# Five groups of transposed tiles ahead of the products, and row sums kept on chip in eight tiles

## The chip, the cores and the metric

The kernel runs on one core of one Trainium2 chip. The metric is the device time of one execution in microseconds; three runs of the kernel before gave 5170.29, 5173.07 and 5176.02 us, median 5173.07 us. A separate, profiled execution took 5216.56 us, and its trace spans 5214.8 us on the core.

## The reference

Two layers on a batch of 32 images of 128 channels and 56 x 56 pixels, all in f32.

```python
# layer 0: depthwise 7x7 convolution, layer norm, a mixture of 8 experts, skips
x = conv7x7_depthwise(input) + bias;  x = layernorm(x) * gamma + beta
topv, topi = top_k(xf @ Wg + bg, 2)          # xf: one row of 128 numbers for each pixel
wts = softmax(topv);  order = argsort(-wts[:, 0])
# in that order each pixel takes a slot in its two experts while they have room (cap)
h = gelu(eb @ W1 + b1);  y = h @ W2 + b2     # per expert, on the rows of its slots
moe = sum over the two slots of gate * y[slot]
return input + x + layer_scale * moe
# layer 1: 3x3 convolution (dilation 3), batch norm, gelu, then in the frequency domain
feat = gelu(batchnorm(conv2d(x, conv_w)))
F2 = fft2(feat);  qkv = F2.reshape(B, 8, 8, N)
attn = softmax over the real part and over the imaginary part of (q conj(k) * tau)
out_f = abs(ifft2(attn @ v))
gate = sigmoid(cg2(gelu(batchnorm(cg1(F2.real))))) * F2
y = concat([out_f, abs(ifft2(gate))]);  return y + x
```

## The kernel before, in words

Layer 0 comes first. The convolution runs on TensorE and leaves normalized rows in the DRAM tensor `xf`; a search finds each expert's threshold; then the eight experts run one after the other, in chunks of 512 rows. A chunk's rows are gathered (L1048), transposed (L1054, L1055), multiplied by W1 (`ph`, L1071) and by W2 (`py`, L1089), scaled, and stored to the DRAM tensor `yf` (L1115). The last expert reads rows that were put in order earlier and has no gathers of its own.

The images of layer 1 are worked in 16 pairs. A pair has seven blocks of eight pixel rows, 112 blocks in all. Before a block can be used, its sum must be made: the block's rows of `xf` (tile `xa`, 448 KB) plus the outputs of the two experts of each pixel, which are gathered from `yf` by 14 indirect DMAs on GpSimd (L458), seven into each of two `y` tiles. Three functions control this.

- `release` (L442) asks for one more gather. Every gather gets a wait on a TensorE instruction: that which was the last when the gather `leash` places before it was asked for. `leash` is 4 in the last expert and 16 in layer 1. The first gather of a block also issues the load of `xa`.
- `total` (L465) makes a block's sum with two VectorE additions (L474). It first asks for what is still missing of the block's 14 gathers. In the kernel before it then stores the sum to the DRAM tensor `xsum` (L475).
- `bring` (L490) makes sure that a block's sum was made, by calling `total` until it is, and in the kernel before loads it back from `xsum` into an `xs` tile (L497), of which there are three.

`release` is called from two places. In the last expert, `ahead` calls it at each tick, for as many blocks as the stored rows of `yf` allow. In layer 1, `worked` counts the columns that TensorE was given and calls `release` once for each `PACE` of 684.2 columns, then `totals(7)`, which makes the sum of a block once seven gathers beyond its own were asked for.

Layer 1 itself has a `front` and a `back` for each pair. `front` takes a block at a time: `place` transposes the block's sum (`pxs`, L1289) and adds it to the padded image (L1293), `bring` is called for the block two further on, and then come 18 of the convolution's matmuls by twos, in three lots of `taps` (`pf`, L1304), and a gelu into `feat` (L1312). `back` makes four transforms, two forward and two inverse. Each calls `transform` (L1339), which works in groups of four tiles: `turn` transposes a group (`pt`, L1347) and VectorE copies it to a `mid` tile (L1334); `product` multiplies the group by a constant matrix (`pm`, L1355) and ScalarE copies the result out (L1358). Three turned groups are made before the first product; from there on one turn and one product take turns. Between the second and the third transform, `attend` makes the attention's products (`pre` and `pim`) and a gate is worked out (`pq`).

The order on TensorE is the program's. While `back` of a pair runs, the main loop feeds it steps of the next pair's `front` in proportion to the columns done, and three lots of taps at a place where a transform needs all of the one before it. Five PSUM banks serve `pt`, `pm`, `pxs`, `pre`, `pim` and `pq` in turn. The `mid` tiles share a pool of six buffers each with the output tiles (`ring`).

Of the kernel before, what the change touches and what calls it, by code (L numbers as in the profile page):

```python
# [30 lines left out]
F32 = mybir.dt.float32  # L31
# [7 lines left out]
C = 128  # L39
# [6 lines left out]
E = 8  # L46
# [5 lines left out]
NB = H // P8  # L52
# [22 lines left out]
def conv_seq_kernel(ctx: ExitStack, tc: tile.TileContext, t: dict, out: bass.AP, dbg: dict):  # L75
# [28 lines left out]

    xf = dram.tile([J * 128, C], F32, name="xf")
    yf = dram.tile([NSLOT + 1, C], F32, name="yf")
    xs_ = dram.tile([J * 128, C], F32, name="xsum")
    xl = dram.tile([-(-cap // 512) * 512, C], F32, name="xlast")
    xfv = xf.rearrange("(j p) c -> p j c", p=128)
    xsv = xs_.rearrange("(j p) c -> p j c", p=128)  # L110
    xlv = xl.rearrange("(j p) c -> p j c", p=128)


# [306 lines left out]
    begun_ = {}  # L420
    marks = []
    leash = {"n": 4}
    made_ = {"asked": 0, "summed": 0, "rows": 0}
    rows = {}
    step = {}
    work = {"since": 0}
# [15 lines left out]
    def release():  # L442

        n = made_["asked"]
        if n >= NRB * NG:
            return
        made_["asked"] += 1
        r, k = divmod(n, NG)
        if k == 0:
            xs = d6.tile([128, NB, C], F32, name="xa", tag="xa")  # L450
            nc.sync.dma_start(out=xs, in_=xfv[:, r * NB : (r + 1) * NB, :])
            begun_[r] = xs, []
        if k % NB == 0:
            begun_[r][1].append(d6.tile([128, NB, C], F32, name="y"))
        m = k % NB
        s = (slot1, slot2)[k // NB]
        marks.append(step["pe"])
        gated(marks[max(0, n - leash["n"])], nc.gpsimd.indirect_dma_start(  # L458
            out=begun_[r][1][-1][:, m, :],
            out_offset=None,  # L460
            in_=yf[: 1 + reach(r), :],
            in_offset=bass.IndirectOffsetOnAxis(ap=s[:, r * NB + m : r * NB + m + 1], axis=0),
        ))

    def total():  # L465

        r = made_["summed"]
        while made_["asked"] < (r + 1) * NG:
            release()
        made_["summed"] += 1  # L470
        xs, ys = begun_.pop(r)
        with tc.issue_after(step["dve"].ins):
            for y in ys:
                nc.vector.tensor_tensor(out=xs, in0=xs, in1=y, op=ALU.add)  # L474
        nc.sync.dma_start(out=xsv[:, r * NB : (r + 1) * NB, :], in_=xs)  # L475

    def totals(lag):

# [9 lines left out]
            totals(NB)  # L488

    def bring(r):  # L490
        if r >= NRB or r < made_["rows"]:
            return
        made_["rows"] = r + 1
        while made_["summed"] <= r:
            total()
        xs = rows[r] = d3.tile([128, NB, C], F32, name="xs")
        nc.sync.dma_start(out=xs, in_=xsv[:, r * NB : (r + 1) * NB, :])  # L497

    def inputs(pr):
        xps = [d4.tile([C, XL], F32, name="xp") for i in range(2)]  # L500
# [24 lines left out]
    if True:  # L525
# [649 lines left out]
        for e in range(E):  # L1175
            todo = late
            chain["on"] = e >= early
            if e + 1 < E:
                todo = todo + [due(1.4, lambda e=e: scale(e + 1))]
            if e in pairs:  # L1180
                todo = todo + search(*pairs[e])
            if e == E - 1:
                for s in late:
                    s()
                locate()
                lists_.close()
                rkey.__exit__(None, None, None)
                d4 = ctx.enter_context(tc.tile_pool(name="d4", bufs=4))
                d6 = ctx.enter_context(tc.tile_pool(name="d6", bufs=6))
                d3 = ctx.enter_context(tc.tile_pool(name="d3", bufs=3))  # L1190
                d0 = ctx.enter_context(tc.tile_pool(name="d0", bufs=1))
                first_inputs = inputs(0)
                bC = load(d0, "beta", [C, 1], t["ln_beta"].rearrange("(c o) -> c o", o=1))
                eps5 = d0.tile([128, 1], F32, name="eps5")
                norms = [[load(d0, n, [128, 5], t[n])] for n in ("bn1", "cgbn")]
                for i, n in enumerate(norms):
                    n += [d0.tile([128, 1], F32, name=f"{k}{i}") for k in ("scale", "shift")]
                cw = load(d0, "cw", [C, 9, DD], t["conv_w"])
                g1 = load(d0, "g1", [128, 32], t["cg1"])
                g2 = load(d0, "g2", [128, 128], t["cg2"])  # L1200
                g2b = load(d0, "g2b", [128, 1], t["cg2_b"])
                tau = load(d0, "tau", [128, 1], t["tau"])
                neg = load(d0, "neg", [128, 128], t["neg"])
                meanw = load(d0, "meanw", [128, 128], t["meanw"])
                rw = load(d0, "rw", [2 * W, 4 * KF], t["rw"])
                rh = load(d0, "rh", [2 * H, 4 * KF], t["rh"])
                ih = load(d0, "ih", [4 * KF, 2 * H], t["ih"])
                iw = load(d0, "iw", [4 * KF, 2 * W], t["iw"])
                todo = []
            if e + 1 < E - 1:  # L1210
                ids2, gates2 = lists()
                steps, late = listing(e + 1, ids2, gates2)
                todo = todo + steps
            elif e + 1 < E:
                (ids2, gates2), late = last, []
            if e == 0:
                todo = todo + search(E - 1, 1)
            if e == early - 1:
                last = [c1.tile([128, NC], d, name=n) for d, n in ((I32, "ids_last"), (F32, "gates_last"))]
                steps, done_ = listing(E - 1, *last)  # L1220
                todo = todo + steps + done_
            slots_ = len(chunks) * 4 - 18
            state = [0, 0, 0.0, 0]
            whole = sum(share.get(f, 0.7) for f in todo)

            def tick():
                state[0] += 1
                if e == E - 1:
                    state[2] += 1
                    ahead(i, state[2])  # L1230
                with tc.issue_after(step["dve"].ins):
                    while state[1] < len(todo) and state[2] * slots_ < state[0] * whole:
                        s = todo[state[1]]
                        if s in apart and state[3] == state[0]:
                            break
                        s()
                        state[2] += share.get(s, 0.7)
                        state[1] += 1
                        state[3] = state[0]

            for i, c0 in enumerate(chunks):
                if i + 1 < len(chunks):
                    then = fetch(ids, chunks[i + 1], e == E - 1)
                elif e + 1 < E:
                    then = fetch(ids2, 0, e + 1 == E - 1)
                if early <= e < E - 1 and i + (e - early) * len(chunks) < NC:
                    put(0, i + (e - early) * len(chunks))
                state[2] = 0 if e == E - 1 else state[2]
                if e == E - 1 and i == len(chunks) // 2:
                    batchnorms()  # L1250
                if e == E - 1 and i == len(chunks) - 1:
                    for r in range(2):
                        bring(r)
                ns, xT = now
                hT, gelu, mine = first_layer(e, ns, xT, tick)
                if left:
                    after, more = second_layer(*left, tick)
                    after(gelu)
                    mine = mine + more
                spots.append(mine + mine[-1:] * (8 - len(mine)))  # L1260
                left = e, c0, gates, ns, hT
                now = then
            assert state[1] == len(todo)
            if e + 1 < E:
                ids, gates = ids2, gates2
# [7 lines left out]
    d1 = ctx.enter_context(tc.tile_pool(name="d1", bufs=1))  # L1273
    d2 = ctx.enter_context(tc.tile_pool(name="d2", bufs=2))
    ring = ctx.enter_context(tc.tile_pool(name="ring", bufs=6))
    psum = ctx.enter_context(tc.tile_pool(name="psum_d", bufs=5, space=PSUM))
    psumf = ctx.enter_context(tc.tile_pool(name="psum_f", bufs=2, space=PSUM))
    psum1 = ctx.enter_context(tc.tile_pool(name="psum_g", bufs=1, space=PSUM))
# [2 lines left out]

    def place(r, xps):
        xs, rb = rows.pop(r), r % NB
        for m0 in range(0, NB, 4):
            nm = min(4, NB - m0)
            pt = bank("pxs")
# [52 lines left out]
    def transform(src, n, m, by, to, copy, more=None):  # L1339
# [3 lines left out]
        def turn(i0):  # L1343
            ni = min(4, n - i0)
            pt = bank("pt")
            for i in range(ni):
                step["pe"] = nc.tensor.transpose(pt[:m, i * 128 : (i + 1) * 128], src(i0 + i), ident)  # L1347
            mid = ring.tile([128, 4, 128], F32, name="mid")
            dve(mid[:m, :ni, :].rearrange("p i c -> p (i c)"), pt[:m, : ni * 128])
            return i0, ni, mid  # L1350

# [12 lines left out]
        for i0 in range(0, n, 4):  # L1364
            turned.append(turn(i0))
            yield turned[-1][1] * 64
            if len(turned) == 3:
                yield product(*turned.pop(0))
        for bank_ in turned:
            yield product(*bank_)  # L1370
# [325 lines left out]
```

## Time and profile before

| | us |
|---|---|
| median of three runs | 5173.07 |
| profiled execution | 5216.56 |
| its span on the core | 5214.8 |
| TensorE busy (matmul) | 4650.3 (89%) |
| GpSimd busy | 2616.5 (50%) |
| VectorE busy | 2816.8 (54%) |
| ScalarE busy | 2079.1 (40%) |
| first gather from `yf` / last | 2604.6 / 5075.6 |
| first `pxs` of layer 1 | 2887.0 |
| first transposes of `feat`, pairs 0, 1 and 2 | 2948.3, 3092.6, 3230.2 |

The DMA queues moved 705.23 MB; 112 stores to and 112 loads from `xsum` of 448 KB each are part of it. A line of the profile's groups names the kernel's line, the engine, the operation and the tiles written and read, then how many there were, their busy time and mean, and what the engine waited for before them. A line of the table of stretches has the stretch, its length, each engine's busy time and number of instructions, the granted TensorE clock, the DMA engines' share and GB/s.

### The profile page before, as it was taken

The numbers are of one execution on the slowest core, as the hardware profiler recorded it, in microseconds if no ns is written. First come the engines' busy times: TensorE is split into PE (matmuls) and PEld (weight loads), VectorE is DVE, ScalarE is ACT, GpSimd is POOL, SyncE is SP. The second block draws the span as 40 slices with busy tenths as digits, with TensorE's granted clock in tenths as the row PEclk, the third lists the DMA queues.
The fourth block names the chain that finished last, engine by engine and source line by source line (L and its number), as shares of the span: only waits on it lengthen the run. The fifth ranks groups of instructions, "written<-read, shape, count | busy, mean of one in ns | idle before, by whom it ended". The sixth has DMA issues, their size and how long they took to land.

```text
span 5214.8 us, 87254 instructions
## 1 busy us (share of the span) xinstructions
PE 4650.3 (89%) x33034; PEld 3232.1 (62%) x33034; DVE 2816.8 (54%) x5863; ACT 2079.1 (40%) x4260; POOL 2616.5 (50%) x2633
## 2 busy tenths in 40 slices
PE   8888845999999999999988899899988888888889
PEld 7777734777776777777766455555555555445556
DVE  4787887868675746442222345455544444444446
ACT  3676751444444444444433133333332222232224
POOL 0000023545555656666366566666666666665650
PEclk9999966999999999999999899999999999998999
DMA  9988840222222323333455456555555555555552
GB/s 255 271 260 262 262 127 26 65 64 66 68 69 71 86 76 85 88 86 93 149 156 133 115 158 163 155 149 149 147 154 152 155 155 158 150 130 146 157 142 57
DMA packets 767737, 705.23 MB, mean 135 GB/s; under 512 B 73232, under 2 KB 679569, under 8 KB 763221
## 3 DMA queue, kind: packets, MB, share of 16 engines
q1 hardware_dynamic: 597060, 487.55, 31.6%
q0 software_dynamic: 81664, 167.15, 14.6%
q10 hardware_dynamic: 88592, 44.96, 3.0%
q8 instruction: 261, 4.28, 0.4%
q14 instruction: 160, 1.30, 0.1%
HBM read 472.99 MB, written 226.39 MB: 134 GB/s over the span
## 4 chain that ended last, share of the span: by engine, by line
PE 70%; another core or an unknown queue 5%; issue 5%; DVE 4%; ACT 2%; DMA 0%; POOL 0%; DVEq 0%; ACTq 0%; POOLq 0%
PE py L1089 16%; PE ph L1071 15%; PE pf L1304 15%; PE pm L1355 9%; PE pt L1347 4%; PE pxt L1054 2%; PE pg L1379 2%; PE pre L1444 2%; PE pxs L1289 2%; PE pim L1445 2%; DVE junk L716 1%; PE pid L956 1%; PE pn L745 1%; DVE mid L1334 1%
## 5 line engine op out<-in xcount | busy, mean ns | idle before, releaser
L458 POOL DMA_INDIRECT y<-yf,slot x1568 | 1552.4, 990 | 971.3 <-issue 357.3
L1048 POOL DMA_INDIRECT xg<-xf,ids x861 | 906.9, 1053 | 689.2 <-PE py L1089 214.7
L1089 PEld LDWEIGHTS py<-W,hT 128*128 128x128 f32 x7872 | 928.9, 193 | 128.6 <-issue 108.2
L1089 PE MATMUL py<-W,hT 128*128 128x128 f32 x7872 | 948.7, 277 | 23.6 <-issue 23.3
L1304 PE MATMUL pf<-xp,cw 128*64 128x448 f32 x4032 | 926.7, 569 | 8.8 <-DVE xp L1293 6.1
L1071 PE MATMUL ph<-xT,W 128*128 128x512 f32 (+1 forms) x1984 | 907.3, 597 | 1.8 <-issue 1.8
L1074 ACT ACTIVATE hT<-ph,b1t 128x512 f32<-128x512 f32 (+1 forms) x992 | 616.2, 672 | 97.7 <-PE ph L1071 52.4
L1334 DVE COPY mid<-pt 112x512 f32<-112x512 f32 (+3 forms) x480 | 311.1, 662 | 570.5 <-PE pt L1347 239.4
L1123 ACT ACTIVATE yo<-yo,gates 128x128 f32<-128x128 f32 x861 | 275.3, 390 | 851.7 <-DVE yo L1103 782.3
L1103 DVE TENSOR_TENSOR yo<-py,b2t 128x512 f32<-128x512 f32 (+2 forms) x256 | 170.6, 669 | 790.1 <-issue 475.0
L1071 PEld LDWEIGHTS ph<-xT,W 128*128 128x128 f32 x1984 | 359.6, 193 | 339.2 <-issue 325.4
L1304 PEld LDWEIGHTS pf<-xp,cw 128*64 128x64 f32 x4032 | 289.8, 140 | 439.0 <-issue 394.7
L220 POOL TENSOR_SCALAR y<-y,sd,nb 128x128 f32<-128x128 f32 x49 | 24.8, 525 | 690.5 <-PE plq L277 689.2
L1358 ACT COPY T<-pm 128x464 f32<-128x464 f32 (+2 forms) x240 | 123.6, 520 | 494.3 <-PE pm L1355 282.6
L225 ACT ACTIVATE y<-y,nb,sd 128x128 f32<-128x128 f32 x735 | 287.6, 481 | 33.4 <-DVE nb L212 33.4
L1293 DVE SCALAR_TENSOR_TENSOR xp<-pxs,beta,xp 128x256 f32<-128x256 f32 x448 | 173.6, 445 | 169.7 <-remote 49.4
L174 PE MATMUL psa<-xt,stay 112*64 112x98 f32 (+1 forms) x4608 | 234.3, 262 | 34.6 <-DVE y L182 16.6
L174 PEld LDWEIGHTS psa<-xt,stay 112*64 112x64 f32 (+1 forms) x4608 | 220.0, 146 | 44.6 <-DVE y L182 23.1
L1312 ACT ACTIVATE feat<-pf,shift,scale 128x448 f32<-128x448 f32 x112 | 81.2, 725 | 411.7 <-remote 141.5
L474 DVE TENSOR_TENSOR xa<-xa,y 128x896 f32<-128x896 f32 x224 | 243.3, 1086 | 2.8
L1355 PE MATMUL pm<-ih,mid 116*128 116x112 f32 x928 | 151.0, 311 | 91.5 <-ACT T L1358 36.6
L1355 PEld LDWEIGHTS pm<-ih,mid 116*128 116x128 f32 x928 | 129.3, 215 | 165.9 <-issue 62.1
(410 smaller groups left out, 6241.9 us busy)
## 6 DMA issues: line engine op xcount, KB each, us to landing
xt<-in_x_dram SPq DMA_DIRECT2D x256, 392.0 KB
yf<-yo SPq DMA_DIRECT2D x240, 256.0 KB
xp<-in_xp_dram SPq DMA_DIRECT2D x32, 1832.0 KB
xa<-xf SPq DMA_DIRECT2D x112, 448.0 KB
xsum<-xa SPq DMA_DIRECT2D x112, 448.0 KB
xs<-xsum SPq DMA_DIRECT2D x112, 448.0 KB
xf<-y ACTq DMA_DIRECT2D x42, 1024.0 KB
y<-yf,slot POOLq DMA_INDIRECT x1568
```

Source lines behind the costliest of these rows:

```text
L174: nc.tensor.matmul(ps[h * 64 : (h + 1) * 64, c * TG : (c + 1) * TG], lhsT=wts[b][:, c4 + c, :], rhs=xv[: PKS[b], c, h, :, b * NB : b * NB ...
L225: nc.scalar.activation(yi, yi, AF.Identity, scale=sd[:, i : i + 1], bias=nb[:, i : i + 1])
L458: gated(marks[max(0, n - leash["n"])], nc.gpsimd.indirect_dma_start(out=begun_[r][1][-1][:, m, :], out_offset=None, in_=yf[: 1 + reach(r), :],
L474: nc.vector.tensor_tensor(out=xs, in0=xs, in1=y, op=ALU.add)
L1048: paced(2 * q, nc.gpsimd.indirect_dma_start(out=xg[:n, q, :], out_offset=None, in_=xf, in_offset=bass.IndirectOffsetOnAxis(ap=ids[:n, c0 + ...
L1071: step["pe"] = nc.tensor.matmul(ph[:, :ns], lhsT=W1[:, e, f * C : (f + 1) * C], rhs=xT[:, :ns], start=True, stop=True)
L1074: gelu = nc.scalar.activation(hT[:, f, :ns], ph[:, :ns], AF.Gelu, bias=b1t[:, e, f : f + 1])
L1089: step["pe"] = nc.tensor.matmul(py[:n, q * C : (q + 1) * C], lhsT=hT[:, f, q * 128 : q * 128 + n], rhs=W2[:, e, f, :], start=(f == 0), sto ...
L1123: nc.scalar.activation(yo[:n, q], yo[:n, q], AF.Copy, scale=gates[:n, c0 + q : c0 + q + 1])
L1304: step["pe"] = nc.tensor.matmul(pf[i * DD : (i + 1) * DD, : 8 * W], lhsT=cw[:, k, :], rhs=xps[i][:, o : o + 8 * RP].rearrange("p (h w) -> ...
L1334: step["dve"] = nc.vector.tensor_copy(to, of)
L1355: step["pe"] = nc.tensor.matmul(pm[:, i * M : (i + 1) * M], lhsT=mid[:m, i, :], rhs=by, start=True, stop=True)
```

## The change

Layer 1's `transform` turns five groups before the first product instead of three, and `mid` tiles get a pool of their own with eight buffers. The sum of a block stays in its `xa` tile, which now comes from a pool of eight (`d9`, in place of six `xa` buffers and three of `xs`): `total` puts the tile into `rows`, and `place` transposes it from there. The store to `xsum`, the load from it and the tensor itself are gone. `release` does nothing when the block of the next gather is eight or more beyond the number of blocks placed; the call is not made up for later. The two early `bring` calls in the last expert are gone, and five one-column tiles of the norms become columns of one tile.

```diff
@@ release
         n = made_["asked"]
-        if n >= NRB * NG:
+        r, k = divmod(n, NG)
+        if n >= NRB * NG or r >= made_["placed"] + HELD:
             return
         made_["asked"] += 1
-        r, k = divmod(n, NG)
         if k == 0:
-            xs = d6.tile([128, NB, C], F32, name="xa", tag="xa")
+            xs = d9.tile([128, NB, C], F32, name="xa")
             nc.sync.dma_start(out=xs, in_=xfv[:, r * NB : (r + 1) * NB, :])
@@ total
                 nc.vector.tensor_tensor(out=xs, in0=xs, in1=y, op=ALU.add)
-        nc.sync.dma_start(out=xsv[:, r * NB : (r + 1) * NB, :], in_=xs)
+        rows[r] = xs
@@ bring
-        if r >= NRB or r < made_["rows"]:
-            return
-        made_["rows"] = r + 1
-        while made_["summed"] <= r:
+        while made_["summed"] <= min(r, NRB - 1):
             total()
-        xs = rows[r] = d3.tile([128, NB, C], F32, name="xs")
-        nc.sync.dma_start(out=xs, in_=xsv[:, r * NB : (r + 1) * NB, :])
@@ the last expert
-                d3 = ctx.enter_context(tc.tile_pool(name="d3", bufs=3))
+                d9 = ctx.enter_context(tc.tile_pool(name="d9", bufs=HELD))      # HELD = 8
...
-                if e == E - 1 and i == len(chunks) - 1:
-                    for r in range(2):
-                        bring(r)
@@ layer 1
+    mids = ctx.enter_context(tc.tile_pool(name="mids", bufs=8))
...
         xs, rb = rows.pop(r), r % NB
+        made_["placed"] = r + 1
@@ transform
-            mid = ring.tile([128, 4, 128], F32, name="mid")
+            mid = mids.tile([128, 4, 128], F32, name="mid")
...
-            if len(turned) == 3:
+            if len(turned) == 5:
                 yield product(*turned.pop(0))
```

More of the change, by code (lines that the diff above doesn't have):

```diff
@@ L106, in conv_seq_kernel @@
     yf = dram.tile([NSLOT + 1, C], F32, name="yf")
-    xs_ = dram.tile([J * 128, C], F32, name="xsum")
     xl = dram.tile([-(-cap // 512) * 512, C], F32, name="xlast")
     xfv = xf.rearrange("(j p) c -> p j c", p=128)
-    xsv = xs_.rearrange("(j p) c -> p j c", p=128)
     xlv = xl.rearrange("(j p) c -> p j c", p=128)
@@ L422, in conv_seq_kernel @@
     leash = {"n": 4}
-    made_ = {"asked": 0, "summed": 0, "rows": 0}
+    made_ = {"asked": 0, "summed": 0, "placed": 0}
+    HELD = 8
     rows = {}
@@ L1193, in conv_seq_kernel @@
                 bC = load(d0, "beta", [C, 1], t["ln_beta"].rearrange("(c o) -> c o", o=1))
-                eps5 = d0.tile([128, 1], F32, name="eps5")
+                five = d0.tile([128, 5], F32, name="five")
+                eps5 = five[:, 4:5]
                 norms = [[load(d0, n, [128, 5], t[n])] for n in ("bn1", "cgbn")]
                 for i, n in enumerate(norms):
-                    n += [d0.tile([128, 1], F32, name=f"{k}{i}") for k in ("scale", "shift")]
+                    n += [five[:, 2 * i + k : 2 * i + k + 1] for k in range(2)]
                 cw = load(d0, "cw", [C, 9, DD], t["conv_w"])
```

## The prediction

> **What bounds the kernel now.** I read the page's rows by slice first, then its groups, then a table of stretches cut at each pair's first transposes of `feat`, and last the timeline at the stalls that the table points to.
>
> ```profile
> PE   8888845999999999999988899899988888888889
> PEclk9999966999999999999999899999999999998999
> ...
> L458 POOL DMA_INDIRECT y<-yf,slot x1568 | 1552.4, 990 | 971.3 <-issue 357.3
> L474 DVE TENSOR_TENSOR xa<-xa,y 128x896 f32<-128x896 f32 x224 | 243.3, 1086 | 2.8
> ```
>
> TensorE is the bound: slices at 8 or 9 from the experts to the end. VectorE's 224 additions waited 2.8 us in all, so the gathers, though 1552 us of GpSimd's time, are never late for them. Yet layer 1 does not run evenly:
>
> ```profile
> 3092.60:3230.20 137.60, 128.38 (x748) 78.11 (x746) 69.61 (x119) 43.65 (x73) 86.88 (x87) 0.95 0.58 157
> 3369.60:3506.70 137.10, 128.09 (x747) 76.20 (x745) 69.26 (x119) 44.03 (x73) 84.91 (x85) 0.95 0.55 151
> 3783.40:3927.10 143.70, 128.41 (x747) 77.04 (x745) 69.59 (x119) 43.44 (x73) 90.29 (x91) 0.95 0.59 158
> 3927.10:4080.90 153.80, 134.42 (x747) 82.15 (x745) 71.32 (x121) 43.73 (x73) 96.35 (x99) 0.91 0.55 146
> 4235.40:4389.50 154.10, 130.98 (x746) 77.75 (x745) 71.06 (x121) 43.23 (x73) 95.63 (x97) 0.92 0.56 148
> 4858.20:5009.80 151.60, 132.33 (x746) 79.11 (x745) 71.33 (x122) 43.85 (x73) 95.90 (x99) 0.94 0.57 154
> 5009.80:5140.50 130.70, 122.72 (x748) 75.27 (x746) 66.95 (x117) 43.64 (x73) 41.32 (x43) 0.97 0.41 112
> ```
>
> Each row is one pair, with the same 746 to 748 matmul records. Pairs 1 to 6 take 137.6, 139.4, 137.1, 139.1, 137.6 and 143.7 us (mean 139.1); pairs 7 to 13 take 153.8, 154.5, 154.1, 156.0, 155.0, 157.7 and 151.6 us (mean 154.7). The step is sharp, between the third and fourth row, and comes with the gathers (the last count of an engine): some 86 to 88 for a fast pair, 97 to 100 for a slow one, 43 in the fastest of all. The timeline shows what a stall looks like, here where the experts end:
>
> ```profile
> 2881.73 0.94 POOL L458 DMA_INDIRECT y<-yf,slot  x1 [0.30 <-issue]
> 2886.21 0.61 DVE L1103 TENSOR_TENSOR yo<-py,b2t 128x256 f32<-128x256 f32 x2 [19.10 <-remote]
> 2886.39 0.94 POOL L458 DMA_INDIRECT y<-yf,slot  x1 [3.72 <-remote]
> ...
> 2886.97 3.82 PE L1289 MATMUL pxs<-ident,xs 128*128 128x128 f32 x17 [21.84 <-DVE yo L1103]
> ```
>
> The last `py` matmul has its record at 2865, but VectorE, which waits for it, starts at 2886.21, when GpSimd has run out of released gathers (twelve back to back, 1.25 us apart, up to 2882.7) and waits itself. The stalls of pairs 7 to 13 have the same look (at 4336 `mid` and `feat` both start after 12.5 us and more, GpSimd having stopped two microseconds before). So: while GpSimd gathers without a pause, TensorE's completions come late; the more gathers per pair, the more of it.
>
> **Why the step is at pair 7.** Count the calls. A pair's yields sum to 27,492 columns in `back` and 31,360 in `front`, 58,852; over 684.2 that is 86.0 releases, while a pair needs 98 (the x85 to x88 of the fast rows). So the lead of the gathers over the blocks placed shrinks by 12 gathers, 0.86 block, a pair. 191 gathers ran before 2887, a lead of 13.6 blocks; the first front loses 3.7 (45.8 releases for 98 placed), less half a block won back before the next; then 0.86 a pair: 10.4, 9.6, 8.7, ... 4.4 at block 56. From block 59 `bring` must ask for what is missing: 98 gathers a pair, and the additions fall directly behind `place` on VectorE. Block 59 belongs to the pair whose front runs beside pair 7's transforms: the step.
>
> **The change, part by part.**
>
> *The cap of eight blocks.* The last expert now stops at 112 gathers, so layer 1 starts with a lead of 8, not 13.6. By the same count it is 4.8 at block 7 and 3.9 at block 14, from where `bring` forces: 84 sums instead of 46. Pairs 1 to 6 turn from fast to slow: 6 x (154.7 - 139.1) = **+94 us**. From above: this. From below: 0, if the slow pairs have another cause. I take the upper end, because of the sharp step at the counted block. Here a rule of the Trainium skill bears ("TensorE: Matmul & The Clock Gate", HAM oscillation): a gap in matmuls of over some 3.4 us halves the clock for the next window. The rows agree in kind: 0.91 to 0.94 in slow pairs, 0.95 and 0.96 in fast ones. If the clock were all, half speed for twice the missing share, a slow pair would lose 154.7 x 0.08 = 12.4 us to it and a fast one 139 x 0.047 = 6.5, a difference of 6 us and +36 us in all; the rest is the gaps before, so the rows' 15.6 us stand.
>
> *What the cap takes out of the last expert.*
>
> ```profile
> 2300.00:2600.00 300.00, 26.89 (x40) 1.00 0.39 109
> 2600.00:2843.60 243.60, 17.13 (x25) 0.92 0.59 152
> ```
>
> These are the copies L1055, one a chunk: 7.5 us a chunk without `yf` gathers, 9.74 us with them. By 2768 there were 111 gathers. In the changed kernel the next 16 are asked for in layer 1 with waits on marks long passed (`leash` is 16 by then), so they run on to about 2768 + 16 x 1.25 = 2788. The 55.6 us from there to 2843.6 shrink to 5.7 x 7.5 = 43: -13. The 21.8 us gap before the first `pxs` has no burst behind it: -20, leaving the 1.5 us of VectorE's sum and its release. **-33 us**; from both sides 0 (the burst only moves) to -45.
>
> *Five groups ahead.* At a transform's start TensorE now has eight more transposes, 8 x 0.11 = 0.9 us, before it needs the first `mid`; the work is the same, moved into what was a wait.
>
> ```profile
> PE pm L1355 <- DVE mid L1334: 73.9, 29, 8.4
> PE pm L1355 <- issue: 41.5, 25, 8.7
> PE pm L1355 <- ACT T L1358: 36.6, 11, 5.6
> ```
>
> 65 waits before `pm`; the most is 65 x 0.9 = 58. In the middle of a transform turns and products share five PSUM banks, so two and a half groups use them up before a third `mid` is missed; nothing is gained there. I take under half, **-25 us**. A loss: five transposed groups hold all five banks, and VectorE needs 5 x 0.69 = 3.5 us for them against 2.2 on TensorE, but the first product needs only the first bank, free at 1.2 us: 0 to +10. At the end of a transform five products follow each other, 0.9 us each, over ScalarE's 0.55: no wait.
>
> *The round trip.* 224 DMAs of 448 KB, 100 MB of 705, leave SP's queue, with its waits for the additions (L475: 463 us) and the loads (L497). Behind them stood the loads of `xa`, asked for four blocks early, and the output stores; no VectorE row waits for those, and `pxs` waited for no load in layer 1. Its cover is the order of blocks: `bring` asks two blocks ahead, some 40 us. **0**; -15 if the freed DMA time shortens the gathers. The load of `xa` into one of eight tiles waits for the placing of a block eight back, but is issued with a lead of four: long done. POOL's queue is unchanged but for the cap. The one-column tiles: 0.
>
> Sum: 5214.8 + 94 - 33 - 25 = 5251, 36 us over the profiled span (5216.56 as that run's own time). The median of the runs shown is 43 us below the profiled run; I carry the difference over: 5173 + 36 = **5209 us**.
>
> **Rivals.** *(a) The slow pairs are not the lead's doing* (a drift in time, say): then only the gains stay, 5173 - 58 = 5115. For it: the stalls' inner cause is inferred; against: the step at the counted block and the return at pair 14, when gathers run out. *(b) The slow pairs come from the round trip*: forced sums are stored and loaded back at once, and SP stands still 3 us each time. Then pairs 7 to 13 become fast too: 5115 - 7 x 15.6 = 5006. Against: no engine waits on what SP issues there. *(c) The sums come onto the path*: VectorE's two additions, 2.2 us, delay the `mid` copies behind each forced block, and stalls lengthen with the clock's halving; for half of 84 blocks that is +92 us, 5300. It decides once a forced addition outlasts the turned groups, which five groups make less likely. *(d) No measurable change*: the cap costs about what the other parts bring, 5163 to 5183.
>
> **How the numbers follow.** My forecast 0.53, its own range 5183 to 5255; (a) 0.18, (b) 0.07, (c) 0.11, (d) 0.11. The range 5115 to 5275 leaves out (b) and most of (c). A measurement tells 0.2% (10 us) from no change; faster: (a), (b) and a little of the forecast's lower edge, 0.28; same 0.11; slower 0.61.
>
> **What would show it.** Right: pairs 1 to 13 all near 154 us with 97 to 100 gathers and a clock of 0.92; 128 gathers or fewer before the first `pxs`, and its gap under 4 us; fewer waits of `pm` for `mid`. Wrong: pairs 1 to 6 near 138 with 98 gathers (a); pairs 7 to 13 near 138 (b); long waits of `pxs` or `pm` for `xa` or `mid` (c).

## The result

| | before | after |
|---|---|---|
| median of four runs, same chip, us | 5171.68 | 5216.82 |
| lowest and highest | 5166.55, 5176.02 | 5212.10, 5226.35 |
| ratio to before | | 1.0092, interval 1.0066 to 1.0117 |
| span of the profiled execution | 5214.8 | 5210.3 |
| first `pxs` of layer 1 | 2887.0 | 2847.8 |
| mean of pairs 1 to 6 | 139.1 | 150.1 |
| mean of pairs 7 to 13 | 154.7 | 151.3 |
| moved by DMA, MB | 705.23 | 602.43 |

The change costs 45 us. The two profiled executions do not show that: their spans differ by 4.5 us the other way, because the profiled run of the kernel before lay 45 us above its own median and that of the kernel after (5212.1 us) did not. So the traces below show where and of what kind the changes are; sizes are taken from runs that were timed side by side. Where in layer 1 the 45 us lie on this chip, the two traces cannot show.

The page of the kernel after, TensorE's row by slice and the groups of the gathers and of the row sums (busy time and mean ns, then the idle time before them). Line numbers of the changed kernel are up to six lower than those of the kernel before:

```profile
PE   7888845999999999999988998889889888888989
...
L457 POOL DMA_INDIRECT y<-yf,slot x1568 | 1546.0, 986 | 984.6 <-issue 368.5
...
L473 DVE TENSOR_TENSOR xa<-xa,y 128x896 f32<-128x896 f32 x224 | 242.9, 1084 | 2.3
```

The dips of TensorE's row, which became steady in the second half of layer 1 (from slice 29, counted from 0), now come from the end of the experts (slice 21) on and last to the end. The additions wait for next to nothing here too, 2.3 us in all. The table of stretches of the kernel after, again cut at each pair's first transposes of `feat`:

```profile
3053.10:3200.90 147.80, 127.21 (x748) 78.15 (x746) 70.75 (x121) 43.62 (x73) 96.36 (x96) 0.93 0.42 111
3350.40:3503.30 152.90, 132.51 (x748) 79.57 (x746) 71.00 (x121) 43.83 (x73) 98.97 (x100) 0.93 0.42 112
3953.90:4108.20 154.30, 135.61 (x747) 81.73 (x745) 70.92 (x121) 43.68 (x73) 96.15 (x98) 0.91 0.40 109
5012.80:5137.90 125.10, 121.02 (x747) 73.00 (x746) 66.29 (x117) 43.70 (x73) 39.38 (x42) 1.00 0.30 78
```

These are pairs 1, 3, 7 and 14. Pair 1 has 96 gathers where it had 87, at a clock of 0.93 where it had 0.95; the shortest pair ahead of pair 14 takes 145.3 us. Pairs 7 to 13, 155 us before, are a little shorter. The timeline of the kernel after where the experts end:

```profile
2847.17 0.95 POOL L457 DMA_INDIRECT y<-yf,slot  x1 [65.31 <-PE py L1083]
...
2847.76 2.05 PE L1283 MATMUL pxs<-ident,xa 128*128 128x128 f32 x17 [0.85 <-DVE yo L1097]
```

GpSimd stood still for 65 us. 112 gathers were asked for in the last expert and then, by the cap, no more; of the next, asked for in layer 1, sixteen ran on up to 2781.9, and the one behind them had to wait for the experts' last product, which was the last TensorE instruction when the 113th was asked for. TensorE's gap before the first `pxs` is 0.85 us where it was 21.84. TensorE's waits from 2700 us on, in us, times and the longest, one of before and two of after:

```profile
PE pt L1347 <- DVE mid L1334: 8.5, 5, 2.8
```

```profile
PE pt L1341 <- DVE mid L1328: 54.8, 11, 13.1
...
PE pm L1349 <- DVE mid L1328: 14.5, 12, 5.0
```

The wait of `pm` for `mid`, 73.9 us before, is 14.5; the wait of `pt` for `mid`, 8.5 us before, is 54.8. The wait for `mid` has moved from the product to the transpose, which needs a free bank.

Place by place the traces give: start of layer 1 -39, pairs 1 to 6 6 x 11.0 = +66, pairs 7 to 13 7 x -3.4 = -24, the rest -8, together -5.

### The profile page after: what moved, and what is told of

It is laid out like the page before. It is cut to its first block, busy times and chain, and to the rows that moved or that the text cites. A ratio compares the mean times of both kernels' runs of the same rounds, so it can differ in the third digit from the quotient of the medians.

```text
span 5210.3 us, 86834 instructions
## 1 busy us (share of the span) xinstructions
PE 4642.1 (89%) x33034; PEld 3225.1 (62%) x33034; DVE 2805.7 (54%) x5863; ACT 2078.4 (40%) x4260; POOL 2616.4 (50%) x2633
## 2 busy tenths in 40 slices
DMA packets 563444, 602.43 MB, mean 116 GB/s; under 512 B 69647, under 2 KB 475280, under 8 KB 558932
## 4 chain that ended last, share of the span: by engine, by line
PE 71%; another core or an unknown queue 4%; issue 4%; DVE 4%; ACT 1%; POOL 1%; DMA 0%; DVEq 0%; ACTq 0%; POOLq 0%
PE py L1083 17%; PE ph L1065 16%; PE pf L1298 14%; PE pm L1349 9%; PE pt L1341 4%; PE pg L1373 2%; PE pxt L1048 2%; PE pxs L1283 2%; PE pre L1438 1%; PE pim L1439 1%; DVE junk L710 1%; PE pid L950 1%; PE pn L739 1%; DVE mid L1328 0%
## 5 line engine op out<-in xcount | busy, mean ns | idle before, releaser
L1306 ACT ACTIVATE feat<-pf,five 128x448 f32<-128x448 f32 x112 | 81.1, 724 | 394.5 <-PE pt L1341 126.0
L180 DVE TENSOR_TENSOR y<-psa,dwbB 128x392 f32<-128x392 f32 x256 | 140.3, 557 | 168.7 <-PE psa L172 125.4
```

## The experiments

They ran on four other chips, and there the program is quicker: the kernel before takes 4780 to 4783 us instead of 5172. So every ratio is to runs of the kernel before on the same chip. TensorE's stalls of the first profile are mostly absent there. Nothing was run again on the first chip, so what these runs show of causes holds for the chips they ran on.

**The kernel before once more.** The same file, to have a trace of it there.

> The kernel before, unchanged, for a second trace. If the trace of before is typical: ratio 1.000, seven slow pairs (7 to 13) near 154 us with 97 to 100 gathers, pairs 1 to 6 near 139 us with 86 to 88, and 191 gathers before the first pxs. What may differ from trace to trace is the length of the gap at the end of the experts (21.8 us in the first trace), since the profiled run there was 44 us above the median of the others.

4783.37 us against 4782.15, ratio 1.0004 (0.9995 to 1.0013). Its pairs: 128, then 119.1 to 121.6 up to pair 8, then 125.6 to 128.5. So the seven pairs of 154 us that were expected did not come: the step is there, two pairs later and half as high. Two rows of its table of stretches (pairs 2 and 10), and from its page the groups of the gathers and of the additions:

```profile
3096.10:3215.20 119.10, 119.10 (x748) 72.90 (x746) 69.22 (x119) 44.03 (x73) 89.96 (x90) 1.00 0.67 183
4067.60:4195.30 127.70, 123.38 (x747) 74.28 (x745) 71.26 (x121) 44.03 (x73) 97.74 (x99) 0.99 0.67 182
```

```profile
L458 POOL DMA_INDIRECT y<-yf,slot x1568 | 1567.7, 1000 | 557.0 <-issue 316.2
...
L474 DVE TENSOR_TENSOR xa<-xa,y 128x896 f32<-128x896 f32 x224 | 243.5, 1087 | 133.1 <-DMA y<-yf,slot 121.4
```

A fast pair is TensorE without a pause at full clock, with 90 gathers beside it, so gathers as such delay nothing that can be seen here. And the additions, which had waited 2.8 us on the first chip, wait 121.4 us for gathers. A gather keeps GpSimd 1.000 us on the mean, and 0.30 to 0.31 us lie between two that follow each other: 1.31 us a gather. At that mean, 98 of them take 128 us and 90 of them 118, which is about what the slow and the fast pairs take.

**The cap alone.**

```diff
-        if n >= NRB * NG:
+        if n >= NRB * NG or n // NG >= made_["placed"] + 8:
...
+        made_["placed"] = r + 1
```

> The kernel before with nothing but the cap: no gather for a block eight or more beyond the blocks placed; three groups ahead and the round trip through xsum stay. Theory (the cap turns pairs 1 to 6 from 86 to 98 gathers): slow pairs 1 to 13, as slow as the changed kernel or slower by what the five groups bring: 5172 + 94 - 33 = 5233 us, ratio 1.008 to 1.014. Rival (the cap is harmless, the loss is from five groups or from the sums on chip): pairs 1 to 6 near 139 us, ratio 0.993 to 1.000.

4806.94 us against 4782.15, ratio 1.0054 (1.0037 to 1.0071), +25 us. Pairs 0 to 3 take 120.5 to 123.1, pairs 4 to 13 mostly 126 to 130. The cap brings the loss by itself, with the store to `xsum` and the load from it still in place. The ratio is below the 1.008 to 1.014 expected, which was worked out from the first chip.

**The changed kernel with three groups** (cap and sums on chip, without the longer lead of the transposes).

```diff
-            if len(turned) == 5:
+            if len(turned) == 3:
```

> The changed kernel with three groups ahead again, cap and sums on chip kept. Theory: five groups save a few us a pair, so this is slower than the changed kernel by 0 to 25 us: 5217 to 5242 us, ratio 1.009 to 1.014. Rival (five groups are the loss): near 5172, ratio 1.000.

4803.49 us, ratio 1.0050 (1.0031 to 1.0069). This too is below what was expected, and above the rival's 1.000. The difference to the cap alone is what the round trip brings, with the pools and the two early calls of `bring` that changed beside it: 3 us, which the intervals (some 8 us each way) do not tell from nothing, for 100 MB less to move.

**Five groups alone** (in the kernel before; `mid` keeps the pool of six).

```diff
-            if len(turned) == 3:
+            if len(turned) == 5:
```

> The kernel before with five groups ahead and nothing else (mid keeps six buffers, one for each group turned and one for the next). Theory: the lead of the gathers is as before (191 by the first pxs, slow pairs 7 to 13 alone) and the five groups save 0 to 25 us: 5147 to 5172, ratio 0.995 to 1.000. Rival (five groups are the loss): ratio 1.005 or more.

4769.57 us, ratio 0.9972 (0.9962 to 0.9982), -13 us. A row of its table of stretches (pair 3):

```profile
3193.50:3311.00 117.50, 117.50 (x747) 72.59 (x747) 68.74 (x120) 44.61 (x73) 90.26 (x90) 1.00 0.66 185
```

Pairs 1 to 7 take 117.2 to 118.6, on the mean 2.5 us less than in the kernel before (117.9 and 120.4); pairs 8 to 14 take 124 to 129, on the mean 1.0 us more (127.4 and 126.5). The saving shows only in pairs that are not at the 128 us of 98 gathers.

**The changed kernel once more.**

> The changed kernel, unchanged, beside the runs on the second chip, where the cap alone gave 1.0054 and five groups alone 0.9972. If the parts add up: 1.0054 x 0.9972 = 1.0026, some 4794 us where before takes 4782; if this chip stalls as the first one does: 1.009 as there.

4804.32 us against 4779.55, ratio 1.0045 (1.0032 to 1.0059). Its pairs 0 and 3 in the table of stretches:

```profile
2839.40:2956.90 117.50, 117.50 (x748) 72.52 (x746) 68.20 (x119) 44.58 (x73) 86.61 (x89) 1.00 0.44 112
...
3194.30:3323.00 128.70, 121.68 (x748) 74.20 (x746) 70.38 (x121) 44.47 (x73) 98.23 (x101) 0.97 0.50 134
```

Against the kernel before on a chip of this kind, layer 1's transforms start 8 us earlier, pairs 0 to 2 are 13 us shorter, pairs 3 to 8 together 45 us longer, pairs 9 to 14 1 us longer and the end 2 us shorter: +23, the difference of the spans. So what is lost shows as six pairs made slow, as many as forecast, of 7.5 us each. It stands in the three-group variant as well: on top of the cap, five groups bring nothing that can be measured (1.0045 and 1.0050), and the parts do not add up to the 1.0026 that was expected of them.

**A faster release, so that the lead is not used up** (99 releases a pair instead of 86), in the changed kernel and in the kernel before with five groups.

```diff
-    PACE = (MAIN + FRONT) / (2 * NP) * 1.07
+    PACE = (MAIN + FRONT) / (2 * NP) * 0.93
```

> The changed kernel with PACE cut from 1.07 to 0.93 of its unit, so that worked asks for 98.9 gathers a pair and bring has nothing left to ask for; the cap of eight stays. Theory A (the number of gathers that GpSimd must run in a pair is what costs): GpSimd has 98 gathers of some 1.30 us = 127 us a pair either way; the lead of five lasts a few pairs longer while 92 a pair are run, so a gain of some 3 to 5 pairs x 7 us = 20 to 35 us against the changed kernel at most. Theory B (it is the place of the additions, directly behind place): all pairs become as fast as pairs 1 to 6 of before, 60 to 90 us faster than the changed kernel on either chip.

> The kernel before (round trip through xsum, no cap, lead of 13.6 blocks) with five groups ahead and PACE 0.93. Theory A: with some 92 gathers a pair run, the lead drains by 6 gathers a pair and is not used up in 15 pairs: the slow pairs go, 6 to 7 x 7 us = 45 us on the second chip, with the five groups' 13 us a ratio of 0.988; on a chip that stalls like the first the gain is smaller, because every pair then has 92 to 98 gathers. Rival (slow pairs have another cause than the lead): 0.997, as five groups alone.

Both expectations missed: 4841.61 us (1.0122, 1.0107 to 1.0138) and 4870.86 us (1.0182, 1.0166 to 1.0198). Most pairs take 128 to 132 us, in the second kernel too, which by the count asks for its gathers some ten blocks ahead as long as any are left. Its pair 2, and what its additions waited for:

```profile
3107.60:3237.30 129.70, 122.47 (x747) 75.65 (x747) 70.50 (x121) 44.12 (x74) 99.83 (x99) 0.96 0.65 179
```

```profile
  DMA y<-yf,slot: 397.9, 89
```

A lead in the program is only a lead in asking. Asked for 99 times a pair, GpSimd falls behind what it was asked for, VectorE meets its two additions before the gathers are done, and behind them in its order stand the `mid` copies that TensorE needs: everything goes at the pace of the gathers. These were over at 4639.5, and TensorE then had 235 us of work left, against 126 us in the kernel before.

**Half of the gathers.** In the kernel before, the rows of each pixel's second expert are left out of the sums, so a block needs 7 gathers.

```diff
-    NG = 2 * NB
+    NG = NB
```

> The kernel before without the gathers of each pixel's second expert (the sum leaves that expert's rows out): 784 gathers instead of 1568, asked for at the same pace, so that they are all run some seven pairs into layer 1. Theory: pairs with gathers take what pairs 1 to 6 of before take on that chip (120 us on the second, 139 us on the first); pairs without gathers show TensorE alone: 117 to 120 us on the second chip, and near 120 on the first too if its stalls belong to the gathers. Rival (the stalls are not the gathers' doing): no difference between the two kinds of pair.

> The kernel before with the rows of each pixel's second expert left out of the sums (7 gathers a block instead of 14), as in half_gathers. On a chip with clock and pairs like those of the first profile (137 to 155 us a pair): if the late completions belong to the gathers, pairs without any gather take 119 to 125 us and those with 90 take near 139; if they belong to the chip, all take near 139. On a chip like those of the other runs: 119 us a pair with and without gathers, 4700 us.

4702.72 and 4703.69 us, on two chips. Two rows of the first one's table of stretches, a pair with gathers and one after the last of them:

```profile
3194.40:3314.00 119.60, 119.60 (x747) 72.95 (x745) 68.73 (x119) 44.33 (x73) 89.95 (x90) 1.00 0.82 232
4269.70:4388.90 119.20, 119.20 (x748) 73.03 (x746) 57.01 (x107) 44.03 (x73) 0.00 (x0) 1.00 0.29 86
```

Ninety gathers a pair and 232 GB/s cost 0.4 us here, and 0.6 us on the mean of pairs 0 to 6. The full kernel takes 77 us more than this one on the same chip: what costs there is not that gathers run beside TensorE, but how many have to be done (and summed, with 112 more additions on VectorE). Neither chip was of the first one's kind, so the question that the second run was for stays open.

**A release pace between the two** (92 a pair), with five groups in the kernel before.

```diff
-            if len(turned) == 3:
+            if len(turned) == 5:
...
-    PACE = (MAIN + FRONT) / (2 * NP) * 1.07
+    PACE = (MAIN + FRONT) / (2 * NP) * 1.00
```

> The kernel before with five groups ahead and PACE 1.00: 92.0 gathers asked for a pair, which is what GpSimd can run beside TensorE's 119 us (92 x 1.30 = 120 us). Theory A (GpSimd's rate is the bound wherever a pair must run 98): the lead of 13.6 blocks drains by 6 gathers = 0.43 block a pair, from about 10 blocks at block 7 to 4 at the end, so no pair is slow: seven slow pairs of 127 to 129 us become 119 to 121, about 50 us below five groups alone, ratio 0.985 to 0.989 on a chip like the second. Rival (more gathers in a pair always cost, as with PACE 0.93): ratio over 1.00.

4767.66 us against 4781.02, ratio 0.9972 (0.9959 to 0.9984): neither the expected gain over five groups alone came nor the rival's loss. The slow pairs are gone as a block, and the same time is spread over all of them (117.5 to 132, mean 123).

**A shorter leash for the gathers in layer 1**, in the changed kernel.

```diff
-    leash["n"] = 16
+    leash["n"] = 4
```

> The changed kernel with a leash of 4 instead of 16 gathers in layer 1, so that GpSimd can be at most four gathers ahead of the place where TensorE asks. On a chip like the second, where GpSimd is the bound in slow pairs: it can no longer fill the stretches where few are asked for, so the same or slower than the changed kernel, 1.004 to 1.02. On a chip like the first, if TensorE's late completions belong to long unbroken runs of gathers: runs are cut to four, the stalls shorten, and it is faster than the changed kernel, by some 10 us a pair.

4818.31 us against 4781.02, ratio 1.0083 (1.0063 to 1.0102): 37 us over the kernel before, where the changed kernel with its leash of 16 is 25 over. GpSimd, which may then run only four gathers ahead of TensorE, stands idle 11 us longer (the table below), and the time goes up by about as much.

**What these have in common** is in the gathers' own rows. For each kernel, from its trace on these chips: what GpSimd stood idle between the first and the last gather from `yf` (all that goes beyond 0.31 us between two), when the last one started, and the span:

| kernel | idle, us | last gather | span | span - last |
|---|---|---|---|---|
| five groups, pace 92 | 4.7 | 4648.9 | 4772.3 | 123 |
| five groups alone | 9.9 | 4644.5 | 4767.5 | 123 |
| before | 25.1 | 4653.1 | 4778.7 | 126 |
| changed, three groups | 51.8 | 4676.5 | 4801.7 | 125 |
| changed | 54.3 | 4681.4 | 4801.7 | 120 |
| cap alone | 55.0 | 4678.5 | 4802.0 | 124 |
| changed, leash 4 | 65.2 | 4694.0 | 4816.1 | 122 |
| changed, pace 99 | 46.5 | 4681.7 | 4843.0 | 161 |
| five groups, pace 99 | 5.0 | 4639.5 | 4874.3 | 235 |

That idle time puts off the last gather is arithmetic. What the runs add is the last column: in seven of the nine the same 120 to 126 us stand behind the last gather, so each us in which GpSimd stands idle is about one us of the end. On these chips it is the bound of the stretch from 2584 on: 1568 gathers at 1.31 us are 2054 us, and 2584 + 2054 + 123 = 4761. The kernel before is 18 us over that sum, and 78 us over the span with half of the gathers. The last two rows lose more at the end because TensorE was held back while the gathers ran.

The hole that the cap makes is seen where layer 1 begins. GpSimd's timeline of the changed kernel, and of the kernel before:

```profile
2747.74 0.94 POOL L457 DMA_INDIRECT y<-yf,slot  x1 [0.30 <-issue]
2783.93 0.94 POOL L457 DMA_INDIRECT y<-yf,slot  x1 [35.24 <-PE py L1083]
```

```profile
2782.36 1.10 POOL L458 DMA_INDIRECT y<-yf,slot  x1 [0.30 <-issue]
2783.76 0.96 POOL L458 DMA_INDIRECT y<-yf,slot  x1 [0.30 <-issue]
```

From 2748.7 to 2783.9 the changed kernel gathers nothing, 35 us, or 27 gathers, while the kernel before goes on without a pause. In all it stands idle 29 us longer, and its span is 23 us longer. On the first chip the same count gives another picture: GpSimd stands idle 440 us in the kernel before and 452 us in the changed one, so its total is not the bound there.

**The test of that.** If GpSimd's total is the bound, taking VectorE's stand before unfinished gathers away must not help beyond 4761 us. The kernel of pace 92 with five groups, and the sum of a block made only when 21 gathers beyond its own were asked for:

```diff
-            totals(NB)
+            totals(3 * NB)
```

> The kernel before with five groups, a release per 639.5 columns, and a block's two additions made only when 21 gathers beyond its own were asked for instead of 7, so that VectorE meets finished gathers. Theory (GpSimd's own total is the bound: 1568 gathers at 1.31 us from the first to the last, about 123 us of work behind the last): the additions' waits (241 us with a lag of 7) mostly go, but the last gather is not before 4640, and the time is that of five groups alone, ratio 0.996 to 0.998. Rival (VectorE standing in front of unfinished gathers is what costs in the slow pairs): pairs with 98 gathers go to about 120 us, ratio 0.985 to 0.990.

4763.19 us against 4780.63, ratio 0.9966 (0.9956 to 0.9977): inside the range of the theory and outside the rival's. The gathers in its trace (ns shortest, median and longest, then first and last start), and what the additions waited for:

```profile
L458 POOL DMA_INDIRECT y<-yf,slot x1568: 938/944/2352, 2585.9 to 4639.8; - x196
```

```profile
  DMA y<-yf,slot: 196.6, 54
```

One part of the expectation missed: the additions still wait 197 us where it was 241. VectorE's stand was hardly taken away, so the run is a weaker test of the rival than it was meant to be. What decides is another number: GpSimd is idle for 3.9 us from the first gather to the last, so no other order of the additions could end these gathers more than 4 us sooner, and the span, 4761.7, is the sum above.

This kernel and five groups alone, whose intervals overlap, beat both the kernel before and the changed one; five groups alone needs one number changed.

## Why the prediction was right, and where it was not

**Direction, size and place held; the size with luck.** 5209 us was forecast and 5216.82 measured, +36 and +45; slower was the likeliest sign, and the range held it. The count of releases (98 needed, 86 made, a lead that starts at eight blocks) said that pairs 1 to 6 would turn slow, and they did on the first chip; on the others it was six pairs as well, 3 to 8. The sum came near because its errors offset each other: the first traces give -5 for the parts where the timed runs give +45, and on the other chips +45 stands for the +94, -8 for the -33 and some -13 for the -25, together about +23.

**The term of +94 was too large.** It measured +66 in the first pair of traces, because pairs 1 to 6 went to 150, not to 154.7: the slow pairs themselves had become 3.4 us shorter. On the other chips it is 6 x 7.5 = +45.

**The reason given for it fell where it could be tested.** "While GpSimd gathers without a pause, TensorE's completions come late" is not what makes a slow pair on the other chips: with 90 gathers a pair TensorE has no pause at all. The slow pairs are those that must have 98 gathers, at 1.31 us each. The step that misled was "the gathers, though 1552 us of GpSimd's time, are never late for them", read from the 2.8 us of the additions and from GpSimd's 50% of the whole span. On the other chips the gathers (1568 us there) and 0.30 us more for each fill the stretch from 2584 us on but for 25 us.

**Whether that is the reason on the first chip too is open.** Its pairs also fit a constant pace of gathers: 139.1 us for 87 and 154.7 for 98 are 1.60 and 1.58 us a gather, and the changed kernel's 151.3 for 98 is 1.54. But there GpSimd was not full; it waited for TensorE's marks. What its gathers waited for (us, times) in the first profile of before, and in the second:

```profile
  PE pm L1355: 143.2, 103
...
  PE pf L1304: 102.3, 59
  PE pt L1347: 98.6, 90
```

```profile
  PE pf L1304: 39.7, 86
  PE pm L1355: 28.2, 75
  PE pt L1347: 19.7, 59
```

So TensorE was behind. The additions waited for gathers on the other chips (121.4 us before, 231.5 us after) and not on the first (2.8 and 2.3 us), so what makes a slow pair on the others was not seen on the chip where the forecast was measured. Why pairs with 98 gathers are slow there is not known. The reading of its stalls was loose as well: nineteen gathers ran back to back before the first of them, not twelve, and near 4336 GpSimd paused twice, with two gathers between.

**What the cap takes out of the last expert** was -33 in the forecast, and -39 in the first traces, with the gap of `pxs` down by 21 as said. The 16 gathers ran on to 2781.9, near the 2788 forecast. On the other chips the kernel before has no such gap (0.92 us), so nothing came back there, and the idle time is loss alone. The step took GpSimd's pause for free because it looked at what TensorE gains from it; it asked of the gathers only when the next 16 would run, not when the last of all would be done.

**Five groups**, -25, measured -13 (9 to 18) alone, on another chip. The 2.5 us that each pair ahead of the step gained would come to 40 over sixteen pairs, more than was forecast; half the pairs stood at the pace of their gathers and passed on none of it. In the changed kernel that is so for pairs 3 to 13, and the gain is gone. The wait of `pt` for `mid`, where `pm` waited before, is what the claim of the five used-up banks would make; no run varied the banks.

**The round trip at 0** is borne out: 3 us, not told from nothing, with 15% of the bytes gone.

**The clock.** The forecast took the lower clock of slow pairs for a consequence of their gaps. Pair 3 of the changed kernel, on the other chips, has one stretch at half clock. TensorE's products around it, and the stretch's row:

```profile
3303.88 1.14 PE L1349 MATMUL pm<-iw,mid 116*128 116x112 f32 x8
3309.49 2.02 PE L1349 MATMUL pm<-iw,mid 116*128 116x112 f32 x8 [4.48 <-DVE ob L1517]
```

```profile
3306.90:3313.70 6.80, 4.21 (x14) 2.55 (x16) 6.47 (x10) 0.53 (x1) 5.28 (x6) 0.50 0.51 120
```

The half clock begins inside the wait of 4.48 us, and the eight products behind the wait take 2.02 us where the eight before it took 1.14. Of the pair's 10 us over a pair that is not at the pace of its gathers (128.7 against 118.5 to 118.9), 7.0 us is time in which TensorE is not busy, and 3 us is longer matmuls. The figure that the forecast took from the Trainium skill's page "TensorE: Matmul & The Clock Gate" (HAM oscillation), gaps of over some 3.4 us, is not a limit in this trace, where a wait of 2.33 us comes ahead of half clock as well; here the measurement decides:

```profile
3401.42 0.65 PE L1341 MATMUL pt<-ident,Z 128*116 128x128 f32 x4 [2.33 <-DVE mid L1328]
```

```profile
3402.50:3405.90 3.40, 3.40 (x13) 1.81 (x13) 3.27 (x7) 1.63 (x3) 2.76 (x3) 0.50 0.51 129
```

**The rivals.** (a), a drift in time, is out: pairs 1 to 6 turned slow in the changed kernel, and on the other chips the cap alone moves the step. (b), the round trip, is out: pairs 7 to 13 of the changed kernel are slow without it, and on the other chips the cap alone is slow with it. (c), sums on the path, was nearest to what the other chips show, with another cause: the additions do stand in front of the `mid` copies, not for their own 2.2 us but for gathers that are not done. (d) is excluded by the interval.

## What to carry to other kernels

Sum an engine's work over the stretch in which it can run, from its first instruction to its last, with the time between two instructions, and set that beside the stretch; a share of the whole span (50% here) hides an engine that is full for its half. When such a producer is the bound, a cap on how far it may run ahead costs what it makes it stand idle, and a lead or a pace at best moves the same time from some pairs to others; too fast a pace (99 a pair) cost 62 us and 91 us. A wait in front of in-order copies shows where the time is lost, but removing it can bring nothing past the producer's own sum. And a cause found on one chip holds for that chip: here the waits that go with slow pairs on the other chips are missing in the traces of the first.

## What the runs showed of the hardware

**Two kinds of chip.** The same program took 5172 us on one chip and 4780 to 4783 on four others. Of the difference of the profiled spans (5214.8 and 4778.7), 103 us lies before the first `pxs` and 333 us behind it. Pair 14, with 43 gathers, took 131 us on the first and 126 (57 gathers) on another, while pairs with 85 to 93 gathers took 137 to 144 and 119 to 122; the last stretch, without gathers, took 74.3 us on both. So most of what the first chip loses in layer 1 it loses where gathers run. From 2700 us on its TensorE ran at half clock for 323 us, against 47 us on the other; if half clock doubles the time of what runs in it, that is some 138 us of the 436, an estimate. Why its completions come late is not known from these runs.

**Gathers and additions.** A gather of 128 rows keeps GpSimd 0.944 to 0.947 us at the median and up to 2.4. In the trace of the kernel before on the second chip, 136 of the 1568 took over 1.2 us. 105 of these ran beside one of the row sums' additions of two SBUF tensors, and 24 more beside the gate's product of two (`Z`). The Trainium skill's "GPSIMD Engine Reference" (Specifications) says that GpSimd's access to SBUF is shared with VectorE, with contention for instructions with two SBUF inputs; the rows agree, though 213 shorter gathers also ran beside an addition. Over all gathers the mean beyond the median comes to some 83 us on GpSimd, which is the bound there.
